# A four-layer graph network: the first layer's products with its weights made inside the adjacency build, and the additions of a stage's sums placed behind the sixth one-hot of the next stage

## The chip, the cores and the metric

The kernel runs on one core of one Trainium2 chip. A core has engines that run side by side, each in the order of its own instructions: TensorE (PE in the profile; its weight loads stand apart as PEld), VectorE (DVE), ScalarE (ACT), GpSimd (POOL) and SyncE (SP), which here only issues transfers (DMAs). They wait for one another through semaphores. Matmul results go to PSUM, eight banks of 512 f32 numbers per partition; everything else lives in SBUF.

The metric is the device time of one execution in microseconds. A kernel's time is the median of its runs.

## The reference, cut to what matters

A graph of 625 nodes with 512 features and 20,000 edges (sorted by receiver, `dst`) passes through four residual layers, each on `relu(layernorm(x))`. Layers 0 and 1 are what the change touches:

```python
def _L0_gnn_ref(x, edge_index, W, b):
    src, dst = (edge_index[0], edge_index[1])
    src_feats = x[src]
    neighbor_sum = jax.ops.segment_sum(src_feats, dst, num_segments=x.shape[0])
    neighbor_count = jax.ops.segment_sum(jnp.ones((src.shape[0],), dtype=x.dtype), dst, num_segments=x.shape[0])
    neighbor_count = jnp.maximum(neighbor_count, 1.0)
    neighbor_mean = neighbor_sum / neighbor_count[:, None]
    h = jnp.concatenate([x, neighbor_mean], axis=-1)
    return h @ W.T + b
```

Layer 1 holds two relational convolutions: for each of four bases, `h @ basis[b]` is gathered over the edges with the weight `comp[etype, b] * norm`, summed by receiver, and `h @ loop_w + bias` is added. Layer 2 is an equivariant convolution with a small network on the edges, layer 3 an edge network of 512 channels. Layers 2 and 3 take most of the time.

## The kernel before

Nodes lie in `NC` = 5 chunks of `P` = 125 rows; edges in 160 tiles of 125. With nodes of 625, layers 0 and 1 need no gathers: the kernel builds dense matrices of 625 x 625 once, the edge counts `cnt` (layer 0) and eight weighted adjacencies `adj` (two convolutions, four bases), and then multiplies by them. Two versions of the body stand in the program; the one for sorted receivers (`layers01_near`) is what runs.

**The build** (up to 170 us in the profile) has `NS` = 16 stages of `GS` = 10 edge tiles. As edges are sorted, a stage reaches only a narrow band of receiver columns. In each stage:

- VectorE makes `rh` twice (L547, the weighted receiver one-hots of five tiles, bf16), and for each tile `ohs` (L556, the sender one-hots of all five chunks; six buffers).
- TensorE (`counted`, L538) adds for each tile and chunk three products into the stage's five PSUM tiles `q`, one per chunk: 150 pairs of weight load and matmul a stage. Eight banks hold `q`, so a stage can start three chunks while the five of the stage before are still being read; its fourth and fifth wait for two of them.
- The sums of a stage go into `adj` and `cnt` at a place read from a register: ScalarE copies the part of the band that no earlier stage reached (`copied`, L517), VectorE adds the 16 columns that overlap (`added`, L527). Before, `copied(s - 1)` and `added` for chunks 0 and 1 stand behind the second one-hot of stage `s`, `added` for chunks 2 to 4 behind the fourth.
- Where a stage enters a new chunk of receiver columns (stages 0, 1, 4, 7, 10), ScalarE first writes zeros to that chunk (`zeroed`, L502, 125x5000 and 125x625 elements).

Stage 0 also makes the edge coefficients (`coefficients`, L461 to L474, and `eq`, L480), in steps between its tiles. `x` is loaded after the first stage (L234; its memory holds the edge types before). In stages 8 and 9 VectorE and ScalarE make the first normalization `h` from it (L242 to L252). The small weights of layer 2 are loaded and scaled in stage 0 (L817 to L830).

**After the build**, layer 0 (L586 to L618): load its two 512x512 weight halves `w0`, transpose `h` (L264), count neighbours by 25 one-column products (`pc`, L595), multiply `h` by the counts (`nsum`, L606, into the transposed sums `sT`), and then make 40 products of `hT` and `sT` with the weights (`l0`, L613), which are added to `x`, the second half scaled by 1/count (L616, L618). Then layer 1: normalize, transpose, load `loop` and four `basis` weights (1 MB each; they can't be loaded before layer 0's memory is free), and multiply (`agg` L637 and L661, `hb` L648).

The order on each engine is mostly that of the code: `keep` (`keep_in_program_order`) fixes it for the build's VectorE and ScalarE instructions; the others, TensorE's among them, are placed by a scheduler. A memory (`tag`) is reused when its readers have ended, and the wait for that is inserted by itself.

Of the kernel before, what the change touches and what calls it, by code (L numbers as in the profile page):

```python
# [9 lines left out]
F32 = mybir.dt.float32  # L10
# [5 lines left out]
N = 625  # L16
E = 20000
D = 512
# [176 lines left out]
def gnn_body(ctx: ExitStack, tc: tile.TileContext, a: dict, out: bass.AP, consts, near: bool):  # L195
# [34 lines left out]
    hT = node.tile([128, KD, N], F32, tag="hT", name="hT")  # L230
# [16 lines left out]
    def norm_relu(h, c, stats, keep=lambda i: i):  # L247
# [4 lines left out]
        nc.scalar.activation(h[:, c, :], x[:, c, :], AF.Relu, bias=off, scale=rstd)  # L252
# [177 lines left out]
    def layers01_near(wts2):  # L430
# [5 lines left out]
        with tc.tile_pool(name="adjacency", bufs=1) as bp:  # L436
            adj = bp.tile([P, NC, NQ, N], F32, name="adj")
            with tc.tile_pool(name="counts", bufs=1) as cp:
                cnt = cp.tile([P, NC, N], F32, name="cnt")
                with tc.tile_pool(name="build", bufs=2) as lp, \  # L440
# [16 lines left out]
                    def coefficients(k0):  # L457
                        ks = slice(k0, min(k0 + 4, K))
                        n = ks.stop - k0
                        oh_r = lp.tile([128, 4, P], F32, tag="oh_r", name="oh_r")  # L460
# [16 lines left out]
                    eq = lp.tile([P, NT, WT], BF16, name="eq", bufs=1)  # L477

# [28 lines left out]
                    def copied(s):  # L507


                        if s in zeros:  # L510
                            zeroed(s)
# [7 lines left out]
                    def added(s, cs):  # L519
# [4 lines left out]
                        for c in cs:  # L524
                            for dst, v in ((adj[:, c, :, at][:, :, lo:hi], done[s][c][:P, :NQ, lo:hi]),
                                           (cnt[:, c, at][:, lo:hi], done[s][c][:P, NQ, lo:hi])):
                                keep(nc.vector.tensor_add(dst, v, dst))  # L527

                    for s in range(NS):
# [14 lines left out]
                        for j0, j1 in zip(parts_of, parts_of[1:]):  # L544
# [6 lines left out]
                            if s == 0 and j1 < GS:  # L551
                                hots(j1, 2 * j1 if j1 < 8 else NT)
                                coefficients(j1)
                            for j in range(j0, j1):
# [10 lines left out]
                                if s > 0 and j == 1:  # L565
                                    copied(s - 1)
                                    added(s - 1, (0, 1))
                                if s > 0 and j == 3:
                                    added(s - 1, (2, 3, 4))
                        if s == NS - 1:  # L570
                            copied(s)
                            added(s, range(NC))
                        if s == 0:
                            load_rest()
                            w2s = layer2_weights(wts2)
                        if s == NS // 2:
                            h = node.tile([P, NC, D], F32, tag="h", name="h")
                            stats = [norm_stats(c, keep) for c in range(NC)]
                        if s == NS // 2 + 1:
                            for c in range(NC):  # L580
                                norm_relu(h, c, stats[c], keep)

                with tc.tile_pool(name="layer0n", bufs=2) as lp, banks("z", 8):
                    w0 = [lp.tile([128, KD, D], F32, name=f"w0{i}", bufs=1) for i in range(2)]
                    for i in range(2):
                        nc.sync.dma_start(w0[i], chunks(a["L0_gnn_W"][i * D:(i + 1) * D, :]))  # L586
                    b0 = lp.tile([P, D], F32, name="b0", bufs=1)
# [1023 lines left out]
```

## Time and profile before

| what | us |
|---|---|
| median of 3 runs | 1818.39 (1816.28 to 1821.70) |
| the profiled execution | 1824.28, its span 1822.5 |
| the build, from the branch on | 11 to 170.3 |
| layer 0 behind it, up to layer 1's first product | 170.3 to 248.6 |
| layer 1's products, TensorE without a break | 248.6 to 589 |
| layers 2 and 3 | 589 to 1822 |
| TensorE busy over the span | 1706.9 (94%) |
| VectorE busy over the span | 1012.5 (56%) |
| mean granted TensorE clock | 0.974 |

A row of the profile names a line of the code, an engine, an operation, `out<-in` with the tiles' names, the shape (partitions x elements), the number of instructions, and their time. "Idle before" is how long the engine stood still before them and what ended it. The chain of waits goes back from the last instruction to what released each step. PEclk, the granted clock, is the share of its full clock at which TensorE was allowed to run.

### The profile page before, as it was taken

What the parts mean: (1) busy time and instruction counts of PE and PEld (TensorE: products, weight loads), DVE (VectorE), ACT (ScalarE), POOL (GpSimd) and SP (SyncE); (2) the same over time, 40 slices, a digit from 0 to 9 for tenths busy, and PEclk for the clock granted to TensorE, in tenths of its full rate; (3) what the DMA queues carried; (4) which work ended last, traced back from release to release, by engine and by line L of the source; (5) the groups of instructions that cost most, each with busy time, mean ns of one, the idle gap of its engine ahead of it and who ended that gap; (6) DMA issues with size and microseconds to landing.
All of it is one profiled execution on the core that took longest, in us unless ns stands there. A gap on an engine that the chain in (4) does not pass through costs nothing.

```text
span 1822.5 us, 24375 instructions
## 1 busy us (share of the span) xinstructions
PE 1706.9 (94%) x9770; PEld 881.2 (48%) x9770; DVE 1012.5 (56%) x1697; ACT 761.5 (42%) x792; POOL 809.1 (44%) x479
## 2 busy tenths in 40 slices
PE   4888999999999888999998899999999999999995
PEld 4878444444444334444454444544444444444443
DVE  7997210001001477877863576776675676667663
ACT  2352110000001312222213667676676777767664
POOL 0000000000000475655625688888887888778300
PEclk9999999999999889999999899999999999999996
DMA  2001030020000384745526478666676666667300
GB/s 73 3 3 54 1 144 0 0 92 6 0 0 0 94 201 136 174 133 160 145 69 162 96 146 169 122 130 109 110 139 111 114 132 121 107 111 140 49 1 13
DMA packets 157219, 162.59 MB, mean 89 GB/s; under 512 B 97546, under 2 KB 104059, under 8 KB 157096
## 3 DMA queue, kind: packets, MB, share of 16 engines
q0 software_dynamic: 131584, 119.48, 33.3%
q1 hardware_dynamic: 20100, 32.69, 5.7%
q10 hardware_dynamic: 5412, 8.77, 1.7%
q8 instruction: 79, 1.29, 0.3%
q14 instruction: 44, 0.36, 0.1%
HBM read 155.11 MB, written 5.12 MB: 88 GB/s over the span
## 4 chain that ended last, share of the span: by engine, by line
PE 87%; DVE 4%; issue 3%; DMA 3%; ACT 2%; DVEq 0%; POOL 0%; another core or an unknown queue 0%; ACTq 0%; POOLq 0%; SPq 0%
PE z L1346 29%; PE agg L661 9%; PE hb L648 8%; PE sum L961 7%; PE q L538 4%; PE tpw L938 4%; PE z L1327 4%; PE z L1332 4%; PE agg L1370 2%; PE xsd L1040 2%; PE agg L637 2%; PE l L613 2%; PE mlp L890 2%; PE nsum L606 1%; PE u L1391 1%
## 5 line engine op out<-in xcount | busy, mean ns | idle before, releaser
L1346 PE MATMUL z<-wm,z 128*125 128x512 f32 x1280 | 558.3, 594 | 2.8 <-DVE z L1465 2.8
L1346 PEld LDWEIGHTS z<-wm,z 128*125 128x125 f32 x1280 | 238.1, 189 | 294.3 <-issue 270.7
L281 POOL DMA_INDIRECT g_s<-xs,src_i x160 | 302.7, 1892 | 129.0 <-issue 75.7
L281 POOL DMA_INDIRECT g_s<-xd,dst_i x144 | 300.8, 2089 | 43.9 <-issue 43.3
L902 POOL MEMSET mT<- 128x5000 f32 x1 | 4.3, 4265 | 587.1 <-PE tr L843 587.1
L281 POOL DMA_INDIRECT gup<-up,src_i x160 | 196.9, 1231 | 128.8 <-DVE msg L945 47.6
L1348 DVE TENSOR_TENSOR mess<-z,b 125x512 f32<-125x512 f32 x160 | 106.4, 687 | 137.4 <-PE z L1346 137.4
L661 PE MATMUL agg<-hb,adj 125*125 125x512 f32 x400 | 173.6, 592 | 0.0
L651 DVE COPY hb<-hb 125x512 f32<-125x512 f32 x20 | 13.8, 692 | 263.3 <-PE hb L648 263.3
L945 DVE TENSOR_TENSOR msg<-tpw,gup 125x768 f32<-125x768 f32 x160 | 151.6, 948 | 0.0
L538 PE MATMUL q<-rh,ohs 125*128 125x96 bf16 (+1 forms) x2400 | 120.7, 213 | 27.5 <-DVE ohs L556 26.3
L1334 DVE TENSOR_SCALAR z<-z,b 128x500 f32<-128x500 f32 (+1 forms) x164 | 108.4, 719 | 59.9 <-PE z L1332 58.2
L1299 ACT ACTIVATE uz<-uz 128x2000 f32<-128x2000 f32 (+1 forms) x41 | 75.0, 1829 | 155.8 <-DVE uz L1291 155.8
L648 PE MATMUL hb<-basis,hT 128*125 128x512 f32 x320 | 138.6, 592 | 0.0
L538 PEld LDWEIGHTS <-ohs 125*128 125x128 bf16 x2400 | 115.8, 101 | 32.6 <-DVE ohs L556 32.3
L961 PE MATMUL sum<-msg,ohy 125*32 125x256 f32 (+2 forms) x1600 | 130.4, 396 | 0.5 <-issue 0.2
L661 PEld LDWEIGHTS agg<-hb,adj 125*125 125x125 f32 x400 | 74.7, 188 | 94.7 <-issue 94.7
L653 ACT COPY hb<-hb 125x512 f32<-125x512 f32 x20 | 11.7, 585 | 260.4 <-PE hb L648 240.5
L961 PEld LDWEIGHTS sum<-msg,ohy 125*32 125x32 f32 x1600 | 75.3, 110 | 90.3 <-issue 66.1
L938 PE MATMUL tpw<-w,hid 64*125 64x512 f32 x320 | 99.1, 653 | 6.8 <-DVE msg L945 6.3
L1299 ACT ACTIVATE um<-um 125x2048 f32<-125x2048 f32 x39 | 74.5, 1910 | 71.1 <-DVE um L1291 71.1
L943 DVE TENSOR_TENSOR msg<-tpw,gup 125x256 f32<-125x256 f32 x160 | 66.8, 417 | 64.3 <-PE tpw L938 32.3
(210 smaller groups left out, 2212.9 us busy)
## 6 DMA issues: line engine op xcount, KB each, us to landing
rt<-in_edge_attr SPq DMA_DIRECT2D x76, 125.0 KB
basis<-in_L_gnn_basis SPq DMA_DIRECT2D x8, 1024.0 KB
gup<-up,src_i POOLq DMA_INDIRECT x160
g_s<-xs,src_i POOLq DMA_INDIRECT x160
g_s<-xd,dst_i POOLq DMA_INDIRECT x144
w<-in_L_gnn_W SPq DMA_DIRECT2D x2, 1024.0 KB
loop<-in_L_gnn_loop SPq DMA_DIRECT2D x2, 1024.0 KB
w1ab<-in_L_gnn_W ACTq DMA_DIRECT2D x1, 2048.0 KB
```

What stands on the lines that cost most here:

```text
L281: return nc.gpsimd.indirect_dma_start(out=dst, out_offset=None, in_=table, in_offset=bass.IndirectOffsetOnAxis(ap=idx[:, t:t + 1], axis=0) ...
L538: nc.tensor.matmul(q[c][:, :n, o:o + WT], hot[j][:, c, :], rhs[j][:, q0:q0 + n, :], start=j + k == 0, stop=j == GS - 1 and k == 2, skip_gr ...
L648: nc.tensor.matmul(p[:P, :], hT[:, k, s * P:(s + 1) * P], basis[b][:, k, :], start=k == 0, stop=k == KD - 1)
L661: nc.tensor.matmul(acc[c], adj[:, s - 1, l * NB + b, c * P:(c + 1) * P], hb[:, b, :], start=False, stop=s == NC and b == NB - 1)
L938: nc.tensor.matmul(p[:P, :], hid[s // 2][s % 2][rws, i * P:(i + 1) * P], w4[rws].rearrange("p k u -> p (k u)"), start=True, stop=True)
L945: nc.vector.tensor_mul(m[:, :, 1:, :], pv[:, 2:4, None, :].to_broadcast([P, 2, 3, MUL]), g[:, None, 1:, :].to_broadcast([P, 2, 3, MUL]))
L961: nc.tensor.matmul(A[r * W:(r + 1) * W, cs, :], oh[:, j, q, :], v, start=j % G == 0 and r not in done, stop=j % G == G - 1, skip_group_che ...
L1299: keep(nc.scalar.activation(u, u, AF.Exp))
L1327: nc.tensor.matmul(pf[f][:, :ne], w[half, f * 128:(f + 1) * 128], rt[half, cols], start=True, stop=False)
L1334: keep(nc.vector.tensor_scalar(zv[:, n, f, :], pf[f][:, :ne], b1[:, f:f + 1], None, op0=ALU.add))
L1346: nc.tensor.matmul(p[:P, :], z[:, j // w, f, j % w * P:(j % w + 1) * P], wm2[:, f, :], start=f == 0, stop=f == KD - 1)
L1348: keep(nc.vector.tensor_add(m[:, j, :], p[:P, :], bc["b2"]))
```

## The change

It does six things.

1. `h` and layer 0's weights are loaded at the start of the build: `x` a second time as `h` (into a tile with one more column of ones, `h1`), `w0b` (the neighbours' half of the weights, in a tile `w2_all` that later holds layer 2's small weights) and `w0a` (the nodes' own half).
2. ScalarE makes the first normalization's statistics in stage 0 (sums and sums of squares by `accum_out`, in place of VectorE's `bn_stats` in stage 8); VectorE takes the reciprocal in stage 0 (`normed`), and ScalarE normalizes.
3. TensorE transposes the chunks of `h` in stage 1 (`turned`), and makes the products of `h` with both weight halves in stages 2 to 10 (`product`), one chunk of one half a stage, its four matmuls behind tiles 4, 6, 8 and 9; the tenth follows the last stage. ScalarE copies each result, over `h` (the neighbours' half) or over the transposed chunk (the own half).
4. All of `added(s - 1)` stands behind the sixth one-hot (`j == 5`).
5. After the build, `cnt` is multiplied with the products instead of with `h`: 50 matmuls of 256 or 257 columns, the last column of ones being the neighbour count. Bias and own half are added to `x` beside it.
6. Layer 1's weights are loaded right after the build; `hb` lies in the memory of the counts. Layer 2's small weights come in stage 8 of the code.

The diff, cut to its core (layer 1's loops, which are only indented and read `hTc`, are left out):

```diff
-                cnt = cp.tile([P, NC, N], F32, name="cnt")
+                cnt_all = cp.tile([P, 2 * NB * D], F32, name="cnt")
+                cnt = cnt_all[:, :NC * N].rearrange("p (c n) -> p c n", c=NC)
+                h1 = node.tile([P, NC, D + 1], F32, tag="h", name="h")
+                h = h1[:, :, :D]
+                hTc = hT_all.rearrange("p (c k n) -> p c k n", c=NC, k=KD)
+                own = hT_all[:P].rearrange("p (c d) -> p c d", c=NC)
+                nc.sync.dma_start(h, a["x"].rearrange("(c p) d -> p c d", p=P))
+                w2_all = wts2.tile([128, KD * D + 448], F32, name="w2_all")
+                w0b = w2_all[:, :KD * D].rearrange("p (k d) -> p k d", k=KD)
+                nc.sync.dma_start(w0b, chunks(a["L0_gnn_W"][D:, :]))
...
+                    w0a = lp.tile([128, KD, D], F32, name="w0a", bufs=1)
+                    nc.sync.dma_start(w0a, chunks(a["L0_gnn_W"][:D, :]))
...
-                        if s in zeros:
+                        if s > 0 and s in zeros:
                             zeroed(s)
...
+                    zeroed(0)
+                    keep(nc.gpsimd.memset(h1[:, :, D:], 1.0))
+                    for c in range(NC):
+                        keep(nc.scalar.activation(h[:, c, :], h[:, c, :], AF.Copy, accum_out=sums[:, c:c + 1]))
+                    keep(nc.scalar.mul(sums, sums, -1.0 / D))
+                    junk = pp.tile([128, 512], F32, tag="q", name="junk")
+                    for c in range(NC):
+                        keep(nc.scalar.activation(junk[:P], h[:, c, :], AF.Square, bias=sums[:, c:c + 1],
+                                                  accum_out=var[:, c:c + 1]))
+                    keep(nc.scalar.activation(var, var, AF.Sqrt, bias=eps, scale=1.0 / D))
+
+                    def normed():
+                        keep(nc.vector.reciprocal(var, var))
+                        keep(nc.vector.tensor_mul(sums, sums, var))
+                        for c in range(NC):
+                            keep(nc.scalar.activation(h[:, c, :], h[:, c, :], AF.Relu, bias=sums[:, c:c + 1],
+                                                      scale=var[:, c:c + 1]))
+
+                    def turned(c):
+                        p = pp.tile([128, 512], F32, tag="q", name="tr")
+                        for k in range(KD):
+                            nc.tensor.transpose(p[:, k * P:(k + 1) * P], h[:, c, k * 128:(k + 1) * 128],
+                                                ident[:P, :P])
+                        keep(nc.scalar.copy(hTc[:, c, :, :P],
+                                            p[:, :KD * P].rearrange("p (k n) -> p k n", k=KD)))
+
+                    products = [(i, c) for i in range(2) for c in range(NC)]
+                    def product(k, at_end=False):
+                        i, c = products[0]
+                        if k == 0:
+                            unit["p"] = pp.tile([128, 512], F32, tag="q", name="hw")
+                        p = unit["p"]
+                        nc.tensor.matmul(p[:P, :], hTc[:, c, k, :P], (w0a if i else w0b)[:, k, :],
+                                         start=k == 0, stop=k == KD - 1)
+                        if k == KD - 1:
+                            keep(nc.scalar.copy((own if i else h)[:, c, :], p[:P, :]))
+                            products.pop(0)
...
+                                if j1 == 8:
+                                    normed()
...
                                     copied(s - 1)
-                                    added(s - 1, (0, 1))
-                                if s > 0 and j == 3:
-                                    added(s - 1, (2, 3, 4))
+                                if s > 0 and j == 5:
+                                    added(s - 1, range(NC))
+                                if s == 1 and j > 4:
+                                    turned(j - 5)
+                                if 2 <= s < 11 and j in (4, 6, 8, 9):
+                                    product((4, 6, 8, 9).index(j))
                         if s == NS - 1:
                             copied(s)
                             added(s, range(NC))
+                            for k in range(KD):
+                                product(k)
                         if s == 0:
                             load_rest()
-                            w2s = layer2_weights(wts2)
-                        if s == NS // 2:
-                            stats = [norm_stats(c, keep) for c in range(NC)]
-                        if s == NS // 2 + 1:
-                            for c in range(NC):
-                                norm_relu(h, c, stats[c], keep)
+                        if s == 8:
+                            w2s = layer2_weights(w2_all)
...
+                    b0 = bias_of(a["L0_gnn_b"], "b0")
+                    weights = layer_weights(0)
+                    with banks("z", 8):
+                        for c in range(NC):
+                            nc.vector.tensor_add(x[:, c, :], x[:, c, :], b0)
+                            nc.vector.tensor_add(x[:, c, :], x[:, c, :], own[:, c, :])
+                        H = D // 2
+                        for c in range(NC):
+                            p = [ps("nsum") for _ in range(2)]
+                            for s in range(NC):
+                                for i in (1, 0):
+                                    nc.tensor.matmul(p[i][:P, :H + i], cnt[:, s, c * P:(c + 1) * P],
+                                                     h1[:, s, i * H:(i + 1) * H + i], start=s == 0,
+                                                     stop=s == NC - 1)
+                            r = rc[:, c:c + 1]
+                            nc.vector.tensor_scalar_max(r, p[1][:P, H:H + 1], 1.0)
+                            nc.vector.reciprocal(r, r)
+                            for i in (1, 0):
+                                xs = x[:, c, i * H:(i + 1) * H]
+                                nc.vector.scalar_tensor_tensor(xs, p[i][:P, :H], r, xs, op0=ALU.mult,
+                                                               op1=ALU.add)
...
-                    for c in range(NC):
-                        for s in range(NC):
-                            nc.tensor.matmul(pc[:P, c:c + 1], cnt[:, s, c * P:(c + 1) * P], ones,
-                                             start=s == 0, stop=s == NC - 1)
-                    sT = lp.tile([128, KD, N], F32, name="sT", bufs=1)
-                    for f in range(KD):
-                        for n0, n1 in ((0, 512), (512, N)):
-                            p = ps("nsum")
-                            for s in range(NC):
-                                nc.tensor.matmul(p[:, :n1 - n0], h[:, s, f * 128:(f + 1) * 128],
-                                                 cnt[:, s, n0:n1], start=s == 0, stop=s == NC - 1)
-                            nc.scalar.copy(sT[:, f, n0:n1], p[:, :n1 - n0])
-                    for c in range(NC):
-                        for i, v in enumerate((hT, sT)):
-                            p = ps("l0")
-                            for k in range(KD):
-                                nc.tensor.matmul(p[:P, :], v[:, k, c * P:(c + 1) * P], w0[i][:, k, :],
-                                                 start=k == 0, stop=k == KD - 1)
```

## The prediction

> **What bounds the kernel now.** I read the busy times by stage first, to find the stretches that the change touches and who fills them. Columns: stretch, its length, busy time (instructions) of TensorE, its weight loads, VectorE, ScalarE and GpSimd, then granted TensorE clock, DMA share, GB/s.
>
> ```profile
> 11.00:46.00 35.00, 20.10 (x268) 19.05 (x269) 27.78 (x64) 11.42 (x14) 0.82 (x1) 0.95 0.22 69
> 46.00:170.30 124.30, 104.71 (x2149) 100.37 (x2146) 116.77 (x329) 50.17 (x159) 0.00 (x0) 0.97 0.01 3
> 170.30:248.60 78.30, 71.94 (x263) 40.45 (x260) 18.41 (x47) 15.48 (x38) 0.00 (x0) 0.93 0.15 50
> ```
>
> From 46.0 to 170.3 (the build's stages 2 to 15) VectorE is busy 94% and TensorE 84%, so TensorE has 19.6 us to spare there. Then 78 us follow in which TensorE works nearly alone. The chain of waits, in order of time, says on what:
>
> ```profile
> 172.89 2.33 PE tr L264 x20
> 175.22 7.79 PE pc L595 x50
> 183.00 24.30 PE nsum L606 x80
> 207.30 34.36 PE l L613 x80
> 241.69 0.76 DVE x L618
> 242.51 5.92 DMA loop<-in_L_gnn_loop
> 248.57 1.99 PE agg L637 x3
> ```
>
> One stage of the build, from the timeline (start, length, engine, line; in brackets the idle time before it and who ended it):
>
> ```profile
> 68.01 4.40 ACT L502 ACTIVATE adj<-iota_f 125x5000 f32<-125x5000 f32 x1 [0.95 <-DVE adj L527]
> 68.27 1.72 DVE L547 TENSOR_TENSOR rh<-eq,parts 125x1500 bf16<-125x1500 bf16 x1
> 69.90 1.56 DVE L556 TENSOR_SCALAR ohs<-iota_s,src_f 125x640 bf16<-125x640 f16 x5
> 70.33 4.36 PEld L538 LDWEIGHTS <-ohs 125*128 125x128 bf16 x96 [1.13 <-DVE ohs L556]
> 70.34 4.50 PE L538 MATMUL q<-rh,ohs 125*128 125x108 bf16 x96 [0.98 <-DVE ohs L556]
> ...
> 75.04 2.62 PE L538 MATMUL q<-rh,ohs 125*128 125x108 bf16 x54 [0.20 <-DVE ohs L556]
> ```
>
> VectorE never rests; TensorE waits for it about 1.2 us per stage, and a pair of weight load and matmul takes 4.36/96 = 0.0454 us. Last, the busy times once more, in three stretches chosen where the granted clock (third number from the end) drops:
>
> ```profile
> 178.10:188.30 10.20, 10.20 (x31) 7.12 (x31) 3.33 (x7) 0.00 (x0) 0.00 (x0) 0.51 0.10 36
> 249.30:252.60 3.30, 3.30 (x5) 1.34 (x4) 0.00 (x0) 0.00 (x0) 0.00 (x0) 0.53 1.04 401
> 109.80:116.30 6.50, 5.78 (x70) 5.78 (x71) 6.46 (x24) 1.23 (x8) 0.00 (x0) 0.50 0.00 0
> ```
>
> After idle gaps of 3.52 us (the timeline, before 110.52) and 2.58 us (before 248.57) TensorE runs at half speed for 6.5 and 3.3 us; gaps of about 1 us do nothing.
>
> **After the build.** Before: from the last one-hot product (170.3) to the first agg matmul (248.57) 78.2 us, and half of the 3.3 us at clock 0.53 behind it, 1.6. After: neighbour sums first multiply by the weights, so 50 matmuls of 256 or 257 columns are left. L613 gives 34.36/80 = 0.43 us for 512 columns and two records a matmul, 0.86; half the columns cost 0.43, together 21.5. pc (7.8) becomes the 257th column. The tail: 0.7 until VectorE has read the last sums (half of L618's 0.75, and the wait), five groups of transposes at 2.1/5 = 0.42, and 0.5 for the copy of the first: 3.3. Its loads (1 MB each) are issued at the build's end; before, loop took 5.9 us from issue, and all five were in after 18 us (DMA 390 to 409 GB/s until 258, after issue at 242.5), so at 21.5 us they are in: the wait of 5.92 us goes. Saved: 79.8 - 24.8 = 55.0 us.
>
> **In the build.** TensorE gets 40 products (34.4 us) and 20 transposes (2.1), more than its 19.6 us of spare time: it becomes the bound of stages 2 to 10. In steps:
>
> - A product stage: 150 pairs x 0.0454 = 6.8, four matmuls x 0.86 = 3.4, and 0.1 for two hand-offs (0.05 from a one-hot's end at 70.28 to the load it releases): 10.35, against 8.25 for VectorE (63.13 to 71.38). The moved additions don't stop this: they need the copies of the stage before, which start when TensorE ends it, and VectorE then has two rh and six one-hots (5.0 us) behind it.
> - Weight loads of f32 (0.19, L613) hide behind f32 matmuls but not behind a pair of 0.045. Between 0 and 0.15 each; I take 0.09, as a bf16 pair hides part: 36 x 0.09 = 3.3.
> - Zeroing. ScalarE runs in order. Before, a chunk is zeroed at once after the additions (68.01, ready by 73.0, as the products end). After, the copy of the product, which waits for TensorE's end of the stage, stands in front of it; in stage 1, the copies of the transposes. So from TensorE's end: 0.1 + copy 0.5 + zeroing 4.3 + 0.7 + first copies 0.46 + first additions 0.4 = 6.5 us until a bank comes free. In the built order 54 pairs (2.45 us) can run meanwhile; TensorE idles 4.0. The stage then takes 6.5 + 96 x 0.0454 + 3.4 = 14.3. This strikes stages 2, 5, 8 (and 11).
> - The layer-2 weights move from stage 0 to stage 6, as their tile is free only then. Before, from w_up's issue (12.70) to w4's last (19.93) 7.2 us, about 2 more to land. Counted from the first product of stage 6, that is 3.3 us after its end (75 pairs and three products, 6.0, lie between). In the built order VectorE's scaling of w4 (0.6) stands ahead of stage 7's additions: what queues behind it are these, and behind them TensorE's banks. TensorE has 45 pairs (2.0) left: idle 2.3. Bounds 0 and 5.
> - Stage 11 has no product, and its first bank is free at 6.5; then VectorE is the bound: four chunks x 0.4 and four one-hots x 0.3, next rh at 9.2.
>
> The sum on the profile's clock. TensorE ended stage 1 at 48.0; 2.1 of transposes come on, 1.4 of VectorE's wait for the sums (40.25) go: 48.7. Stages 2, 5, 8: 42.9. Six others: 62.1. w4: 2.3. Loads: 3.3. End of stage 10: 159.3. Stage 12 begins 9.2 later, 168.5, and as before takes 35.4 to the end (134.94 to 170.3): 203.9. The last product: 207.3.
>
> Clock: each 4.0 us gap is as long as those that halved the clock. One drop costs half of 3.3 to 6.5 us, 1.6 to 3.2; a gap can also lie such that nothing happens. Four gaps between 0 and 12.8; I take 6. [...]
>
> So the build ends at 213.3, agg starts at 213.3 + 24.8 = 238.1 instead of 250.2 (248.57 and the 1.6): **12 us less**.
>
> **What I cost at nothing.** The new statistics: x's load moved 128 GB/s and took 10 us, so h, issued at 11, lands about 23; five copies and five squares at 0.58 to 0.81 (L653, L252), a table load of 1.28 and small ones are done at 30.7 to 33. VectorE reads them at about 34: hidden by the coefficients. Its two new operations (0.17 each) replace the w4 scaling there. [...] VectorE loses 4.0 (104.49 to 108.48) and 1.3 us (116.07 to 117.41) of norm, which counts no more where TensorE is the bound. VectorE's ten additions to x (6.2 us) run under the first sums. Layer 1's products and everything behind are the same instructions.
>
> The profiled execution has a span of 1822.5 and 1824.28 in all, 5.9 above the median; I take the difference over: 1818.4 - 12 = 1806. About 0.3% (5.5 us) is what a measurement can tell from no change.
>
> **Rivals.**
>
> - *TensorE takes the products better than I say* (1793 to 1799): no clock drop (-6), no exposed loads (-3), w4 in time (-2): 1795. For: gaps of 1 to 2 us didn't gate the clock. Against: 4.0 us is longer than both gaps that did. 0.15.
> - *The load of h comes late* and the gain goes there: h, w0b and w0a leave the same queue at once. If they share the 128 GB/s that x's load got, 3.3 MB take 26 us; h lands at 39, the statistics end at 48, and VectorE stands 14 us in stage 0: 1820. For: x's load used only a third of the engines. Against: the two w loads at 172 to 178 moved 249 to 393 GB/s together, and h is first. Half of it, 7 us, is enough for no measurable change. 0.20.
> - *The clock gate makes it slower*: after each of the five gaps (stages 2, 5, 7, 8, 11) the half clock lasts 10.2 us as from 178.1 to 188.3, since a product stage has small waits in it: 5 x 5.1 = 25.5 instead of 6, 1826. It decides from about 47 us at half clock on (23.5 us lost). For: that stretch was busy throughout, and still slow. Against: it follows 50 one-column matmuls, which none of these stages has; 110 to 116 shows 6.5 us. 0.13.
>
> **How the numbers follow.** The forecast has 0.52 and its own range is 1799 to 1813: between all bounds of loads (0 to 5.4), w4 and clock, but not all at one end. Faster: 0.52 + 0.15, less a little of the upper edge, 0.66. Same: 0.20. Slower: 0.14, with a late h beyond its price. The range 1796 to 1823 leaves out the slow rival and half of the quick one's lower edge.
>
> **What would show it.** nsum 50 matmuls in 21.5 us and agg starting near 238; TensorE idle some 4 us before the first pairs of chunk 3 in stages 2, 5, 8, 11, released by VectorE's additions, and ScalarE's zeroing right behind the product's copy; 10.3 us a stage in 3, 4, 6, 9, 10; VectorE waiting for a DMA at w4's scaling. Wrong, if product stages take 12 us or more, if VectorE waits for ScalarE at the reciprocal in stage 0, or if agg waits for loop.

## The result, and the profile after

The changed kernel takes 1809.77 us (median of 9 runs, 1806.36 to 1816.67), the kernel before 1817.07 on the same chip (9 runs): a ratio of 0.9959, with a 95% interval of 0.9943 to 0.9976. It is faster by 0.4%, some 7 us; the forecast was 1806, with a range of 1796 to 1823. The profiled execution took 1808.68, its span 1806.9. The variants below ran on four chips on which the kernel before takes 1798 to 1802; each ratio is to runs of the kernel before on the variant's own chip. On one of these chips the changed kernel stood at 0.9948 (0.9932 to 0.9964).

The ratio is known to about 0.2% (3 us) either way. The profile is sharper: everything that the change touches lies before the first agg matmul. Before, it started at 248.57, with 1.6 us lost to half clock behind it (250.2 in effect); now it starts at 240.0 at full clock. That is 10.2 us less, and the first matmul of layer 2's tables, much later, comes 9.9 us earlier (579.15 for 589.05). What else differs between profiles lies in layers 2 and 3, which did not change.

The busy times of the changed kernel in the three stretches that answer to those shown of before (columns as there; the build is now 11 to 214):

```profile
11.00:56.00 45.00, 26.64 (x393) 25.62 (x394) 32.77 (x72) 25.47 (x47) 0.83 (x2) 0.92 0.39 112
56.00:214.00 158.00, 139.83 (x2132) 113.41 (x2128) 110.54 (x312) 50.78 (x167) 0.00 (x0) 0.95 0.03 7
214.00:240.00 26.00, 23.75 (x117) 20.38 (x117) 16.75 (x48) 6.03 (x12) 0.00 (x0) 1.00 0.62 222
```

The 78 us behind the build have become 26. The build is 44 us longer, and TensorE, which had 16% of it to spare, is now busy for 88%. The chain of waits, in order of time (start, length, what), says what lies between:

```profile
35.94 1.28 ACT L555
...
91.63 4.39 ACT adj L516
97.53 2.68 PE q L598 x30
...
116.23 2.47 DMA w_all<-in_L_gnn_W_mlp
120.75 1.88 PE q L598 x38
...
210.57 3.51 PE hw L583 x8
214.14 5.79 DMA b<-in_L_gnn_b
...
238.19 1.98 PE tr L691 x16
240.16 2.58 PE agg L706 x6
```

The square root's table load stands on the chain in stage 0, a zeroing of 4.39 us before each of four groups of pairs (91.63 is one), and layer-2 weights at 116. No wait for loop is left at the end. Behind the build the chain goes by the load of layer 0's bias (214.14) and VectorE's additions behind it; VectorE takes the last sums at 236.78, TensorE ended them at 236.66, so this way is hardly longer than TensorE's own. The timeline of the changed kernel (start, length, engine, line; in brackets the idle time before it and who ended it):

```profile
28.28 0.63 ACT L549 ACTIVATE h<-h 125x512 f32<-125x512 f32 x1 [10.91 <-PE q L598]
37.57 0.19 DVE L558 RECIPROCAL var<-var 125x5 f32<-125x5 f32 x1 [3.89 <-ACT var L555]
38.32 10.32 PE L598 MATMUL q<-rh,ohs 125*128 125x108 bf16 x180 [7.08 <-DVE ohs L618]
...
73.13 1.08 PE L583 MATMUL hw<-w_all,hT 128*125 128x512 f32 x2
74.05 1.51 PE L598 MATMUL q<-rh,ohs 125*128 125x108 bf16 x30
...
83.86 1.08 PE L583 MATMUL hw<-w_all,hT 128*125 128x512 f32 x2
...
90.94 2.85 PE L598 MATMUL q<-rh,ohs 125*128 125x108 bf16 x54
91.14 0.59 ACT L586 COPY h<-hw 125x512 f32<-125x512 f32 x1 [8.31 <-PE q L598]
91.62 4.40 ACT L516 ACTIVATE adj<-iota_f 125x5000 f32<-125x5000 f32 x1
...
97.53 2.68 PE L598 MATMUL q<-rh,ohs 125*128 125x108 bf16 x30 [3.73 <-DVE cnt L541]
...
119.65 0.36 DVE L902 TENSOR_SCALAR w_all<-w_all 128x384 f32<-128x384 f32 x1 [1.88 <-DMA w_all<-in_L_gnn_W_mlp]
120.75 1.88 PE L598 MATMUL q<-rh,ohs 125*128 125x108 bf16 x38 [0.88 <-DVE cnt L541]
...
190.41 6.95 PE L598 MATMUL q<-rh,ohs 125*128 125x108 bf16 x150 [0.36 <-DVE ohs L618]
198.03 6.95 PE L598 MATMUL q<-rh,ohs 125*128 125x108 bf16 x150 [0.67 <-DVE ohs L618]
...
214.79 21.87 PE L676 MATMUL nsum<-h,cnt 125*125 125x257 f32 x100 [0.72 <-issue]
```

Four things are to be seen. In stage 0, ScalarE first touches h at 28.28, and VectorE stands 3.89 us at the reciprocal. From 73.13 to 83.86 an undisturbed stage with products takes 10.73. In stage 5 the zeroing stands right behind the product's copy, and 54 pairs are all that TensorE has until 97.53. The same gap comes in stages 2, 8 and 11 (3.64, 3.73, 3.74). In stage 7 VectorE waits 1.88 us for the layer-2 weights, and TensorE 0.88 for VectorE. The busy times around this one (granted clock third from the end) show what follows it:

```profile
96.00:98.00 2.00, 0.47 (x6) 0.45 (x7) 0.99 (x6) 2.00 (x11) 0.00 (x0) 0.84 0.00 0
98.00:100.00 2.00, 2.00 (x27) 2.00 (x25) 1.98 (x10) 0.43 (x3) 0.00 (x0) 0.50 0.00 0
100.00:102.00 2.00, 2.00 (x21) 1.24 (x19) 2.00 (x4) 0.00 (x0) 0.00 (x0) 0.80 0.00 0
```

### The profile page after: what moved, and what is told of

It is laid out like the page before. It is cut to its first block, busy times and chain, and to the rows that moved or that the text cites. A ratio compares the mean times of both kernels' runs of the same rounds, so it can differ in the third digit from the quotient of the medians.

```text
span 1806.9 us, 24315 instructions
## 1 busy us (share of the span) xinstructions
PE 1702.6 (94%) x9740; PEld 881.9 (49%) x9740; DVE 1009.8 (56%) x1692; ACT 769.2 (43%) x811; POOL 812.3 (45%) x480
## 4 chain that ended last, share of the span: by engine, by line
PE 88%; DVE 4%; ACT 3%; issue 2%; DMA 1%; POOL 0%; DVEq 0%; ACTq 0%; another core or an unknown queue 0%; POOLq 0%; SPq 0%
PE z L1419 29%; PE agg L730 10%; PE hb L717 8%; PE sum L1034 7%; PE q L598 5%; PE tpw L1011 5%; PE z L1405 4%; PE z L1400 4%; PE mlp L963 2%; PE agg L1443 2%; PE hw L583 2%; PE xsd L1113 2%; PE agg L706 2%; PE u L1464 1%; PE o L1495 1%
## 5 line engine op out<-in xcount | busy, mean ns | idle before, releaser
L282 POOL DMA_INDIRECT g_s<-xs,src_i x160 | 297.8, 1861 | 127.6 <-issue 75.6
L282 POOL DMA_INDIRECT g_s<-xd,dst_i x144 | 307.3, 2134 | 43.9 <-issue 43.6
L730 PE MATMUL agg<-cnt,adj 125*125 125x512 f32 x400 | 173.6, 592 | 0.0
L720 DVE COPY cnt<-hb 125x512 f32<-125x512 f32 x20 | 13.8, 690 | 256.2 <-PE hb L717 256.2
L598 PE MATMUL q<-rh,ohs 125*128 125x96 bf16 (+1 forms) x2400 | 127.8, 215 | 29.3 <-DVE cnt L541 15.7
L598 PEld LDWEIGHTS <-ohs 125*128 125x128 bf16 x2400 | 122.5, 102 | 54.1 <-issue 34.7
L730 PEld LDWEIGHTS agg<-cnt,adj 125*125 125x125 f32 x400 | 74.8, 188 | 94.7 <-issue 94.7
L722 ACT COPY cnt<-hb 125x512 f32<-125x512 f32 x20 | 11.7, 585 | 253.5 <-PE hb L717 253.5
L1011 PE MATMUL tpw<-w_all,hid 64*125 64x512 f32 x320 | 99.8, 653 | 0.1
```

The lines of the kernel that those rows point to most:

```text
L282: return nc.gpsimd.indirect_dma_start(out=dst, out_offset=None, in_=table, in_offset=bass.IndirectOffsetOnAxis(ap=idx[:, t:t + 1], axis=0) ...
L598: nc.tensor.matmul(q[c][:, :n, o:o + WT], hot[j][:, c, :], rhs[j][:, q0:q0 + n, :], start=j + k == 0, stop=j == GS - 1 and k == 2, skip_gr ...
L730: nc.tensor.matmul(acc[c], adj[:, s - 1, l * NB + b, c * P:(c + 1) * P], hb[:, b, :], start=False, stop=s == NC and b == NB - 1)
L1011: nc.tensor.matmul(p[:P, :], hid[s // 2][s % 2][rws, i * P:(i + 1) * P], w4[rws].rearrange("p k u -> p (k u)"), start=True, stop=True)
```

## The experiments

In the diffs, indentation is taken off and `...` stands for lines left out. "In effect" adds what half clock cost behind the first agg matmul.

| kernel | first agg at | median us | ratio to before (95%) |
|---|---|---|---|
| before | 248.6 (250.2 in effect) | 1798 to 1802 | 1 |
| changed, again | 241.4 | 1792.6 | 0.9948 (0.9932 to 0.9964) |
| zeroing ahead | 217.7 | 1772.4 | 0.9831 (0.9810 to 0.9851) |
| additions at the old places | 254.7 | 1808.4 | 1.0030 (1.0016 to 1.0044) |
| normalizations at the end of stage 0 | 236.2 | 1790.1 | 0.9925 (0.9902 to 0.9947) |
| all products after the build | 225.1 | 1779.1 | 0.9870 (0.9846 to 0.9895) |
| before, additions moved alone | 237.6 | 1790.3 | 0.9930 (0.9909 to 0.9951) |
| gaps filled | 233.6 | 1785.5 | 0.9913 (0.9895 to 0.9931) |
| gaps half filled | 236.3 | 1791.3 | 0.9936 (0.9919 to 0.9953) |
| weights behind h | 237.4 | 1788.9 | 0.9925 (0.9908 to 0.9942) |
| before, one wait per addition | 250.0 (251.7 in effect) | 1801.2 | 1.0015 (0.9999 to 1.0032) |
| zeroing ahead, late norm, late w4 | 213.4 | 1763.3 | 0.9787 (0.9769 to 0.9804) |
| zeroing ahead, late norm, products after | 215.8 | 1766.4 | 0.9810 (0.9791 to 0.9829) |

**The changed kernel again**, unaltered.

> The changed kernel itself, unaltered, on the chip that the variants ran on, since times of the kernel before differ by 0.8% between the two chips. If ratios carry over, it stands at 0.996 (0.994 to 0.998) of before and agg starts at 240 (239.5 to 240.5); if not, the variants' ratios can be compared only with this one.

The variants ran on this chip and three others. Ratios carry over within their intervals; agg at 241.42 is outside what was expected and lies 1.4 us behind the first profile, so landmarks are good to about that. (Stage 1 ended 0.8 earlier here, at 52.57, but TensorE ran slowly for longer behind the gap of stage 2: the first product's two records took 2.04 us at 61.56 and the 21 pairs behind them 1.84, against 1.51 at 62.39 and 1.11 in the changed kernel.) Differences to the changed kernel below are to 240.0.

**Zeroing ahead.**

```diff
 def copied(s):
-    if s > 0 and s in zeros:
-        zeroed(s)
...
 zeroed(0)
+zeroed(1)
...
     added(s - 1, range(NC))
+    if s > 1 and s in zeros:
+        zeroed(s)
```

> The zeroing of a chunk's columns moves ahead by most of a stage: chunk 1 at the start with chunk 0, chunks 2 to 4 right behind the additions of the stage before, so that no product's copy stands in front. My theory (the zeroing behind that copy is what TensorE waits for): the four idle gaps of 3.6 to 3.7 us before chunk 3's pairs in stages 2, 5, 8 and 11 go, and with them the half clock behind each. Stages 2, 5 and 8: 3 x 3.7 + about 6.8 of clock; stage 11, where VectorE is the bound, about 1; sum 19. The first agg matmul starts at 221 (217 to 225) instead of 240.0, the time is 19 us (16 to 22) under the changed kernel, about 1791. The half clock of 36 to 42 in stage 0 and the wait in stage 7 stay. Rival (the gaps only show time that VectorE or the banks would take anyway): the idle time reappears elsewhere in the same stages, agg starts at 237 or later and the time stays within 3 us of 1809.8.

agg starts at 217.68, 22.3 earlier than in the changed kernel, near the upper edge of the gain that was expected. All four gaps are gone. The timeline of this kernel around stage 5:

```profile
77.22 4.41 ACT L516 ACTIVATE adj<-iota_f 125x5000 f32<-125x5000 f32 x1 [0.35 <-DVE adj L539]
...
84.97 3.80 PE L597 MATMUL q<-rh,ohs 125*128 125x108 bf16 x75
85.17 0.59 ACT L585 COPY h<-hw 125x512 f32<-125x512 f32 x1 [2.93 <-PE q L597]
85.65 0.38 ACT L529 COPY adj<-q 125x256 f32 x1
```

The zeroing runs in ScalarE's idle time ahead of the product's copy. Behind that copy the sums are copied at once, and TensorE goes on without a break (x75 instead of x54 and a wait).

**Gaps filled, and half filled.** Zero weights are multiplied while TensorE waits; the wait itself stays. `NF` is 66:

```diff
+none = lp.tile([P, 128], BF16, name="none", bufs=1)
+keep(nc.gpsimd.memset(none, 0.0))
...
     for jj in range(3):
         counted(jj, cs)
+    for i in range(NF if s in (2, 5, 8, 11) and 0 in cs else 0):
+        nc.tensor.matmul(q[2][:, :NQ, :WT], none, rhs[0][:, :NQ, :],
+                         start=False, stop=False, skip_group_check=True)
```

> The changed kernel, with 66 pairs of zero weights (they add nothing to the sums) set in front of the waiting pairs of stages 2, 5, 8 and 11: the wait for the banks stays, but TensorE is busy for 3.0 of its 3.7 us. Tells the half clock apart from the wait itself. Theory: the granted clock stays at 1 in these four places, and the 8.4 us of clock lost in the 2-us windows behind the gaps (1.6, 1.7, 3.4, 1.6) come back, less 1 to 1.6 in stage 11, where VectorE is the bound: agg at 233 (231 to 235) instead of 240.0. Rival (the clock's fall hits work that has slack, as the rivals of small effect would have it): agg at 238.5 or later. Other rival (the clock falls for another reason than idle time, for instance the products): the windows still show 0.50.

agg at 233.61, 6.4 us earlier. With 0.84 to 0.94 us idle in these four places instead of 3.64 to 3.74, the granted clock is 1.00 in the windows around them (56 to 72, 94 to 104, 130 to 146, 170 to 182) instead of 0.79 to 0.89: the half clock behind these gaps came from the idle time, and it was on the path. With `NF` at 33:

> As with the gaps filled by zero pairs, but 33 instead of 66, 1.5 us, so that 2.2 us of the wait stay idle in one piece. Tells how long an idle stretch must be. If the clock falls after each, agg starts at 239 to 240 as without filling; if after none, at 233.6 as with 66. Idle stretches of 2.58 us (kernel before) and 1.72 (weights behind h) were followed by half clock, one of 1.71 (zeroing ahead) was not; if only the place of the stretch decides below 3.5 us, some of the four fall: 235 to 238.

agg at 236.32, between the two. The timeline of this kernel, and then its busy times:

```profile
59.01 1.53 PE L601 MATMUL q<-rh,ohs 125*128 125x108 bf16 x30 [2.24 <-DVE cnt L544]
...
95.09 1.82 PE L601 MATMUL q<-rh,ohs 125*128 125x108 bf16 x30 [2.33 <-DVE cnt L544]
```

```profile
60.00:62.00 2.00, 2.00 (x30) 1.43 (x28) 2.00 (x8) 0.01 (x1) 0.00 (x0) 1.00 0.03 8
...
96.00:98.00 2.00, 2.00 (x16) 1.32 (x14) 2.00 (x8) 0.00 (x0) 0.00 (x0) 0.53 0.03 8
```

In stage 2, 2.24 us of idling left the clock alone; 2.33 halved it in stage 5, as did 2.33 and 2.34 in stages 8 and 11 (0.50 from 134 to 136 and from 172 to 174). The length alone does not decide it: the last section has stretches of equal length that were and were not followed by half clock.

**Additions at the old places**, in the changed kernel.

```diff
     copied(s - 1)
-if s > 0 and j == 5:
-    added(s - 1, range(NC))
+    added(s - 1, (0, 1))
+if s > 0 and j == 3:
+    added(s - 1, (2, 3, 4))
```

> Only the additions go back to their old places behind the second and the fourth one-hot; the products stay in the build. My theory: VectorE then stands at the second one-hot of every stage until ScalarE has copied the first chunks, and TensorE, which has 45 pairs at most in hand, idles at each stage's start for 1.2 to 2.4 us, which hurt nothing while VectorE was the bound but adds to every stage where TensorE is: 9 product stages x 1.2 to 2.4, 11 to 22, I take 16; agg starts at 256 (251 to 262), the time is about 1826. Rival (the place of the additions does not matter, since they need the stage before in either place): agg starts within 3 us of 240 and the time stays near 1810.

agg at 254.65, 14.7 later; the kernel is then 0.3% slower than before. Without the moved additions, all that the products and the new sums bring is a loss of 4.5 us (254.65 against 250.2). The timeline of TensorE in this kernel:

```profile
184.77 4.28 PE L598 MATMUL q<-rh,ohs 125*128 125x108 bf16 x57 [5.32 <-DVE cnt L541]
...
197.50 7.26 PE L598 MATMUL q<-rh,ohs 125*128 125x108 bf16 x150 [0.98 <-DVE ohs L618]
205.76 7.56 PE L598 MATMUL q<-rh,ohs 125*128 125x108 bf16 x150 [0.99 <-DVE ohs L618]
```

The four gaps are 5.2 to 5.3 us instead of 3.6 to 3.7, an undisturbed stage with products takes 11.48 (between the last products of stages 9 and 10, 165.77 and 177.25) instead of 10.73, and the stages that VectorE bounds stand 8.26 apart instead of 7.62: 4 x 1.6, 6 x 0.75 and 4 x 0.64 make 13.4 of the 14.7. The other half of the question is the move by itself:

**The kernel before, with the additions moved alone.**

```diff
     copied(s - 1)
-    added(s - 1, (0, 1))
-if s > 0 and j == 3:
-    added(s - 1, (2, 3, 4))
+if s > 0 and j == 5:
+    added(s - 1, range(NC))
```

> The kernel before with one part of the change alone: all ten additions behind the sixth one-hot, everything else as it was. Theory, formed from the four runs before (without products the stages went 7.6 us apart instead of 8.25, and five chunks' additions took 1.40 instead of 1.9 to 2.0 us): behind the second and fourth one-hot each addition waits for ScalarE's copy of its chunk, 0.40 apart; behind the sixth the copies are done and they run 0.28 apart. 14 stages x 0.6 is 8.4, and the wait of 1.43 in stage 1 goes: the last one-hot product ends 9 us earlier (7 to 11), the first agg matmul starts near 239.5 instead of 248.6, ratio 0.995. Rival (VectorE has the same work in either order and was never at rest, as the prediction had it): within 1.5 us of before, ratio 0.999 to 1.001.

The transposes behind the build start at 162.25 instead of 172.89, agg at 237.58; ratio 0.993. These few lines give at least as much as the whole change. Why, if VectorE "never rests"? The timeline of VectorE, first before, then in the changed kernel's stage 13, where no product is made:

```profile
75.20 0.29 DVE L527 TENSOR_TENSOR adj<-q,adj 125x128 f32 x1
75.41 0.17 DVE L527 TENSOR_TENSOR cnt<-q,cnt 125x16 f32 x1
75.60 0.29 DVE L527 TENSOR_TENSOR adj<-q,adj 125x128 f32 x1
75.81 0.17 DVE L527 TENSOR_TENSOR cnt<-q,cnt 125x16 f32 x1
76.00 0.29 DVE L527 TENSOR_TENSOR adj<-q,adj 125x128 f32 x1
```

```profile
197.90 0.28 DVE L541 TENSOR_TENSOR adj<-q,adj 125x128 f32 x1
198.09 0.16 DVE L541 TENSOR_TENSOR cnt<-q,cnt 125x16 f32 x1
198.18 0.28 DVE L541 TENSOR_TENSOR adj<-q,adj 125x128 f32 x1
198.37 0.16 DVE L541 TENSOR_TENSOR cnt<-q,cnt 125x16 f32 x1
198.46 0.28 DVE L541 TENSOR_TENSOR adj<-q,adj 125x128 f32 x1
```

The instructions are equally long, but a chunk takes 0.40 us before and 0.28 after, from start to start; what differs is the space between cnt and the next adj. Five chunks: 0.6 a stage. The stages that VectorE bounds are 7.62 apart (190.41, 198.03, 205.65) instead of 8.25. The expectation's reason for it was wrong: ScalarE had copied the last chunk by 75.37, and the additions of 75.60 and 76.00 waited for no copy.

**The kernel before, with one wait for each addition.**

```diff
+    keep(nc.vector.memset(last[:1, NC - 1, :1], 0.0))
     added(s - 1, (0, 1))
...
+last = hot[-1]
 if s == 0:
```

> The kernel before, its additions left at their old places, with one tiny write of VectorE ahead of them that waits for TensorE's last pair of the stage before. In the program before, every chunk's first addition waits for two semaphores, TensorE's and ScalarE's; in the changed kernel and in the one with the additions moved alone, a one-hot ahead of them has already waited for TensorE, and 75 of 80 carry ScalarE's alone. Here the tiny write takes that wait, and again 75 of 80 carry one. Theory (the second wait costs 0.12 a chunk even when it is long met: chunks 2 to 4 were copied by 75.4 and their additions still stood 0.40 apart): those three chunks go 0.28 apart, the first two at ScalarE's 0.34; 0.3 to 0.45 a stage less the tiny write, 14 stages: the last one-hot product ends 4 us earlier (2.5 to 6), ratio 0.998. Rival (the place decides: ahead of the copies VectorE must wait for them, whatever the number of semaphores): 0.40 stays, end within 1.5 us or later, ratio 1.000 to 1.001.

The rows of `added` in the trace bear the expectation's counts out. In the kernel before, each of the 80 chunks has a semaphore instruction more; in the changed kernel only the five of the last stage have, and there the chunks stand 0.40 apart too (210.52, 210.92, 211.31). The two lines are of before and of the changed kernel:

```profile
L527 DVEq EVENT_SEMAPHORE  x80: 21/21/21, 39.7 to 172.3; - x80
```

```profile
L541 DVEq EVENT_SEMAPHORE  x5: 21/21/21, 210.1 to 212.0; - x5
```

The timeline of VectorE in this kernel:

```profile
75.28 0.06 DVE L567 MEMSET ohs<- 1x1 bf16 x1 [0.27 <-PE q L538]
75.79 0.29 DVE L527 TENSOR_TENSOR adj<-q,adj 125x128 f32 x1 [0.45 <-ACT cnt L517]
...
76.99 0.28 DVE L527 TENSOR_TENSOR adj<-q,adj 125x128 f32 x1
77.19 0.17 DVE L527 TENSOR_TENSOR cnt<-q,cnt 125x16 f32 x1
77.27 0.28 DVE L527 TENSOR_TENSOR adj<-q,adj 125x128 f32 x1
```

The mechanism holds for the distance: at the old place, with the tiny write ahead of them, chunks 2 to 4 stand 0.28 to 0.30 apart. The time does not follow: in front of the first addition 0.27 and 0.45 us of waiting have come up, stages take 8.55 (69.59 to 78.15), and the kernel is no faster. So two things count, the second semaphore and the place: behind the sixth one-hot the wait for TensorE has been met by the one-hots, and neither it nor the copies hold VectorE up (the additions from 197.90 to 198.46 have no idle time in front of them). The second wait costs about 0.12 us a chunk here: 0.40 where the trace has the semaphore row, 0.28 where it has none.

**Normalizations at the end of stage 0.**

```diff
-    if j1 == 8:
-        normed()
...
 if s == 0:
+    normed()
     load_rest()
```

> The reciprocal and the five normalizations go from the middle of stage 0 to its end, behind the last one-hot. My theory (h landed about 5 us later than forecast, and VectorE stands 3.9 us for the square root, behind which TensorE idles 7.1 us and falls to half clock): the wait of 3.89 us at the reciprocal goes, stage 1 ends 4 to 5 us earlier, and every later landmark with it: agg at 235.5 (234 to 237), time 4.5 us lower, about 1805. Rival (stage 0 has slack for it, or the wait moves to the transposes of stage 1): agg stays at 239 or later and the time within 2 us of 1809.8.

agg at 236.17, 3.8 earlier: the wait was on the path.

**First-layer weights issued behind h.**

```diff
-nc.sync.dma_start(w0b, chunks(a["L0_gnn_W"][D:, :]))
...
-nc.sync.dma_start(w0a, chunks(a["L0_gnn_W"][:D, :]))
...
 keep(nc.scalar.activation(var, var, AF.Sqrt, bias=eps, scale=1.0 / D))
+keep(nc.scalar.dma_start(w0b, chunks(a["L0_gnn_W"][D:, :])))
+keep(nc.scalar.dma_start(w0a, chunks(a["L0_gnn_W"][:D, :])))
```

> The two loads of first-layer weights are issued by ScalarE behind the square root instead of on SyncE's queue right behind h, so that h shares its time with the small ea load alone. Theory (the weights' 2 MB made h late): ScalarE's first copy of h starts at 23 (22 to 25) instead of 28.28, VectorE's wait of 3.89 at the reciprocal is gone, agg starts at 236 (235 to 237.5). Rival (h's own load takes 17 us wherever the weights are): the first copy stays near 28, agg near 240.

The first copy of h starts at 24.04 instead of 28.28, and VectorE's wait is gone: the two weight loads had made h some 4 us late. agg comes 2.6 us earlier (237.38), 1.4 less than expected. One visible part is stage 7: TensorE's gap there is 1.72 us now, instead of 0.88, and is followed by half clock (0.50 from 118 to 120).

**All products after the build**, and the same with the zeroing ahead and the late normalizations (its edit is those three together).

```diff
-    if 2 <= s < 11 and j in (4, 6, 8, 9):
-        product((4, 6, 8, 9).index(j))
 if s == NS - 1:
     copied(s)
     added(s, range(NC))
-    for k in range(KD):
-        product(k)
+    while products:
+        for k in range(KD):
+            product(k)
...
-if s == 8:
-    w2s = layer2_weights(w2_all)
...
+w2s = layer2_weights(w2_all)
 with banks("y", 3):
```

> All ten products with the weights stand behind the last stage, none in the build; the layer-2 weights are loaded after the sums. Tells what hiding the products in the build buys. My theory: the stages fall back to VectorE's 8.25 us (122.3 us from stage 1's end to stage 15's before, less 5.3 of norm, which no longer runs on VectorE), so that from 53.8 the build ends at 171, or 174 with the one gap that stays in stage 2, and the products follow with 40 x 0.86 = 34.4: 205 to 209 against 214.1 for the changed kernel with only one product left at the end. agg starts at 233 (230 to 237), the time is 7 us lower (3 to 10), near 1803: hiding them as it is done loses more by gaps and half clock than it hides. Rival (the hiding works as it should and saves most of the 30.9 us of the nine hidden products): the build alone ends at 195 or later, agg starts at 255 or later and the time is 15 us or more above the changed kernel.

agg at 225.11, 15 us before the changed kernel; the expectation had 230 to 237, since it still sized VectorE's stages at the old 8.25. As the change stands, the products inside the build cost more than they hid. And against the kernel before with the additions moved alone (237.58), the new sums with no product hidden bring 12.5 us. With the zeroing ahead and the late normalizations:

> All products behind the last stage, with the zeroing ahead and the normalizations at the end of stage 0: what hiding the products is worth once no gap is left. Theory: from the run with all products after the build (agg at 225.1) the wait in stage 0 (3.8), the gap in stage 2 (3.6) and its half clock (1.6) go, less where VectorE takes over: agg at 217 (215 to 219), 3.6 us behind the candidate with hidden products (213.4), ratio 0.981. Rival (hiding is worth most of the 30.9 us of nine products, and only the gaps ate it): agg at 225 or later.

agg at 215.77, as forecast. Against this, hiding them is worth 2.3 us at agg in the candidate that follows. In both, stage 1 ends at the same time (49.74 and 49.76) and TensorE runs at full clock from there on (1.00 from 56 to 187.5 in the candidate; here 6.95 us for 150 pairs in each stage from 66.67 to 142.86, as in the changed kernel at 190.41), so that this isn't the chance of the clock. The medians differ by 3.2, but they are of two chips, and the intervals of the ratios overlap.

**The candidate**: zeroing ahead, late normalizations, and the scaling of w4 behind the additions of stage 12.

```diff
-if s == 8:
+if s == 12:
     w2s = layer2_weights(w2_all)
...
-nc.vector.tensor_scalar_mul(w4[:, :3, :], w4[:, :3, :], s4)
-nc.vector.tensor_scalar_mul(w4[:, 3, :], w4[:, 3, :], s4 / math.sqrt(3.0))
+tc.keep_in_program_order(nc.vector.tensor_scalar_mul(w4[:, :3, :], w4[:, :3, :], s4))
+tc.keep_in_program_order(nc.vector.tensor_scalar_mul(w4[:, 3, :], w4[:, 3, :], s4 / math.sqrt(3.0)))
```

> A candidate: the zeroing ahead (217.7 with this alone), the normalizations at the end of stage 0 (3.8 with this alone) and the scaling of w4 behind the additions of stage 12 (the idle 1.71 in stage 7): if the three add up, agg starts at 212.2 (211 to 214) and the ratio is 0.980. If the wait only moves to the transposes of stage 1 or to another chunk, 214 to 217.7.

agg at 213.44, ratio 0.9787: 2.1% faster than before, and well ahead of the changed kernel. Its busy times in the build:

```profile
56.00:187.50 131.50, 128.41 (x2073) 104.29 (x2071) 104.74 (x296) 46.38 (x155) 0.00 (x0) 1.00 0.03 9
```

TensorE is busy for 98% at full clock. Zeroing (22.3) and normalizations (3.8) make 213.9 together, so the late w4 added 0.4 to 0.5 of the 1.7 hoped for, less than two profiles of one kernel differ by.

## Why the prediction was right, and where it was not

- **After the build**: right. nsum takes 21.87 (forecast 21.5), the way from its end to agg 3.3 as forecast, and loop's wait is gone. From the end of the build to agg 25.9 against 24.8.
- **A product stage**: 10.73 measured, 10.35 plus 0.36 of weight loads forecast. A product between pairs takes 0.92 (73.13 to 74.05), so 0.06 is exposed where 0.09 was taken.
- **Zeroing**: right in place and mechanism, 3.64 to 3.74 idle where 4.0 was forecast; the run with the zeroing ahead shows it, and shows it as the costliest flaw of the change (22.3 us).
- **Clock**: 6 forecast, 6.4 shown on the end by the filled gaps. From stage 1's end (53.4) to stage 10's (168.25) 114.9 us passed; the forecast, with three quarters of its clock term, gives 115.1.
- **w4**: 2.3 forecast, 0.88 measured (0.7 to 1.7 in the other profiles that kept it in stage 7), within its bounds.
- **Statistics costed at nothing**: wrong, 4.7 us. Stage 1 ended at 53.4, not 48.7. The load of h landed 5 us later than the 23 taken from x's load; 4.2 of these go when the weights are issued behind it. The statistics then took 9.3 us to the square root's end, within the 7.7 to 10 forecast (the table load among them 1.28, with the square root right behind it at 37.24), so VectorE stood 3.9 us, and TensorE's idle 7.1 brought half clock (0.50 from 35.93 to 42.76). The rival of the late h was right in kind, and a third of its 14 us.
- **Stages 11 to 15**: wrong by 3.9 in the other direction. From stage 10's end to the last product the forecast had 44.6 and 1.5 of clock, measured 42.2. It took 35.4 for stages 12 to 15 "as before" and 0.4 for each chunk's additions, so it missed that the moved additions make VectorE's stage 0.6 shorter. For the move it had only the 1.4 us of VectorE's wait in stage 1.

The last two misses all but cancel by luck, which is why agg came within 1.9 us of the forecast 238.1. The picture behind the number was lopsided: it had the gain come from the new sums and the earlier products, but without the moved additions these end 4.5 us behind the kernel before, whatever they save behind the build. What is left as gain is about that of the moved additions, which the forecast had at 1.4 us: 13 us in effect on the kernel before (250.2 to 237.6), 13 to 15 in the changed one (254.7 to 241.4 or 240.0). The new sums were worth 12.5 us more (237.6 to 225.1), and hiding the products, as it was done, lost 15 (225.1 to 240.0). In the kernel before it is the shorter stage of VectorE, 0.6 x 14 = 8.4, the wait of 1.43 in stage 1, and the end at full clock. In the changed one it is mostly shorter gaps and shorter product stages, as the run with the additions at the old places shows.

Of the rivals, the quick one needed no loss of clock, and there were four; the slow one needed 47 us at half clock, and about 17 were there behind the four gaps (8.4 lost, read from windows of 2 us).

## What to carry to other kernels

Work moved onto an engine with spare time makes that engine the bound, and then each small wait that cost nothing before (a zeroing behind a copy, a load that shares its queue's time) comes on the path, with the clock's loss on top (6.4 us here); look for those waits first, since the candidate that mends three of them gave 29 us on top of the change's 9, nearly all of it by the zeroing and the statistics. An engine whose rows stand close together can still be waiting: compare the starts of equal instructions in two places, not their lengths. A change of several parts should be measured part by part, in both directions: here a few moved lines gave some 13 us, another part 12, and a third lost 15, while the whole showed only the 10 that were left.

## What the runs showed of the hardware

- From 31 us to layer 1's first products, TensorE's granted clock was 0.50 from 34.45, 109.54, 177.81 and 249.49 on in the kernel before, for 3.41, 6.83, 10.24 and 3.41 us, and from 35.93, 59.83, 97.37, 134.92 and 175.88 on in the changed kernel, for 6.83, 3.41, 3.41, 6.83 and 3.41 us; in between it was 1.00. The one of 177.81 began while TensorE was busy with the one-column products of pc (175.22 to 183.00). In both profiles the starts lie whole multiples of 3.41 us apart (22, 20 and 21 times it before; 7, 11, 11 and 12 times after).
- Half clock came with idle stretches of TensorE of 2.58, 2.77 and 3.52 us (before), 3.64 to 3.74 and 7.08 (changed kernel), 2.33 and 2.34 (gaps half filled) and 1.72 (weights behind h). It did not follow 2.06 us (before, ahead of 172.89; 1.00 until 177.81), 2.24 (gaps half filled, stage 2), 1.71 (zeroing ahead, 1.00 from 110 to 116) and 0.84 to 0.94 (gaps filled). Two variants have a stretch of 2.77 us that ends at almost the same time: in the candidate (34.04) the clock from 34 to 46 was 0.76; with the products after the build (34.05) the 90 pairs behind it took 4.22 us, which is full speed. So the length of a stretch does not decide by itself between 1.72 and 2.77 us; what else does, these runs do not show.
- The additions of `added` stood 0.40 us apart, chunk to chunk, where the trace has an event-semaphore row of 21 ns for each chunk (80 in the kernel before; five in the changed kernel, all in its last stage), and 0.28 where it has none (stage 13 of the changed kernel): about 0.12 us a chunk, in the kernel before also for the chunks whose copies were long done (copies by 75.37, additions at 75.60 and 76.00).
- ScalarE's sums over a row in the changed kernel (L549, L553) appear as two instructions, one of 0.61 to 0.69 us over 512 elements and a read-out of 0.18 to 0.19 us.
- A load was read later when more was issued behind it on the same queue: h (1250 KB) 13.0 us after its issue with 312.5 KB behind it (weights behind h; issue at 11.07, first read at 24.04), and 17.2 us with 2048 KB of weights and the same 312.5 KB behind it (changed kernel; 11.06 and 28.28).
